# Moving layer-norm work of two batches between the attention stages and the MLP stage of a cross-attention block

## The chip, the cores and the metric

The kernel runs on one core of a Trainium2 chip. The metric is the device time of one execution in microseconds. Several executions are timed; the median is compared.

## The reference

A transformer block on x (4 batches x 512 rows x 512) with a context of the same shape, all in float32: layer norm 1, cross attention of 16 heads of width 32 with a mask, an output projection with residual, layer norm 2, an MLP of inner width 2048 with tanh-gelu, and a second residual.

```python
x = layer_norm(hidden_states, ln1_w, ln1_b)
q = heads(x @ q_w + q_b); k = heads(ctx @ k_w + k_b); v = heads(ctx @ v_w + v_b)
scores = where(mask, einsum('bhqd,bhkd->bhqk', q, k) * scale, min)
out = einsum('bhqk,bhkd->bhqd', softmax(scores), v)
hidden = merge(out) @ cproj_w + cproj_b + hidden_states
y = layer_norm(hidden, ln2_w, ln2_b)
return hidden + gelu(y @ fc_w + fc_b) @ proj_w + proj_b
```

## The kernel before

**Stages.** Attention is cut into 16 stages w = 4b + g, one per batch b and group g of four heads, and each stage into four units qt = 0 to 3 of 128 query rows. A unit is numbered u = 4w + qt, so stage 11 holds units 44 to 47 and stage 13 units 52 to 55. In a unit, `scores` (lines 255 to 272) makes four 128x512 score blocks on TensorE in one tile `sc` that has one buffer; VectorE adds the mask and takes the row minimum `mn` of the negated scores (line 266); ScalarE takes exponentials into `ptt` (line 270). `turn` (line 274) transposes 32x32 blocks into `tb` on VectorE (lines 285, 293, 294).

**Exchange.** Two units make a pair, numbered 2w + half. After a pair's second unit SP issues 16 transfers that finish the transposition between partitions (line 328). Pairs 25, 27, 29 and 31 land in the space of `xe`, pairs 1, 3, 5 and 7 in that of `gt`, and all others in the single buffer `pT`: the transfers of such a pair are issued only when the pair before it in `pT` has been attended. `attend` (line 331) multiplies the probabilities with v on TensorE (line 345, `av`) and normalises on VectorE (line 350, `oT`), after which a held pair may be issued. A pair is attended some units after it was made: pair 22 in unit 48, pair 23 in unit 50, pair 24 in unit 53, pair 26 in unit 57, pair 27 in unit 59.

**The order is written by hand.** The kernel uses a manual schedule: each engine executes in the order of the program text. Lists `first[w]` give the work that stands behind each unit; where it is a tuple, entry qt stands behind unit 4w + qt. In a unit come, in this order: attend (if due), scores, turn, the listed work. Such work is the k, q and v projections (`A`, lines 218 to 245), the output projection (`C`, line 386, with the residual addition on VectorE at line 387), layer norm 2 and parts of the MLP of earlier batches, which `some(n)` takes from one list in order: first layer pairs `fc` (line 528) and second layer tiles `proj` (line 536).

**Layer norm 2** of a batch has four parts. `stat2` takes mean and variance of a 128x512 tile on VectorE (lines 128, 129), `ln_rs` the inverse root on POOL (lines 134, 136), `norm2` subtracts and scales on VectorE (line 150), and `ln2_turn` transposes on TensorE (line 159) and applies weight and bias (lines 162, 164) into `yT`.

**Seven products.** The MLP replaces 8 block products by 7 (a Strassen-Winograd form), for which sums of blocks are needed: `y_sums` makes four 128x512 sums of `yT` on VectorE (line 452), into `ys` and in place; the weights' sums `wsum` are made on POOL during attention, and on VectorE behind it (`sum_wa`, lines 452 and 455 on `gt`). `fc_seven` (line 479) multiplies (line 491), copies one block p on ScalarE (line 494), adds the blocks on VectorE (line 455) and applies gelu on ScalarE (line 509). Gelu and the exponentials need different function tables, so ScalarE loads a table at each change.

**Bias rows.** `proj_bias` adds the second MLP bias to the residual tiles that stay on chip (batch one: two of four tiles) on POOL (line 357). `c_bias` does so with the projection's bias.

**Behind attention** `last_mlps` (line 575) runs the second half of batch one's MLP (first layer pairs c = 4 to 7), then all of batch two's and three's. Per pair: sums of the next pair's weights, seven products, the load of the weights after next; `g_sums` makes sums of gelu's outputs for every two pairs. In `project` the second layer follows; the transposes of the next batch's layer norm 2 (`turns2`) stand between its second and third product. Within batch two's first layer the kernel takes batch three's statistics and normalisations, by this block:

```python
if b == B - 2:
    for t in {0: (0,), 1: (1, 2), 3: (3,)}.get(c, ()):
        stat2(b + 1, t)
```

The lists that the change touches read before:

```python
first[11] = (..., t2[2:] + do(lambda: y_sums(1)) + pb_(1) + some(1) + h_(2, 2, 3, 0, 1))
first[13] = some(1), some(1) + stat(2, 0, 1), some(1) + stat(2, 2, 3) + rs(2), some(2)
first[14] = some(1) + norm(2, 0, 1), norm(2, 2, 3) + some(2), some(2), []
```

Of the kernel before, what the change touches and what calls it, by code (L numbers as in the profile page):

```python
# [52 lines left out]
def xattn_block(ctx: ExitStack, tc: tile.TileContext, x, encT, mask, q_w, k_w, v_w, c_w, fc_w, p_w, vecs, rows, out):  # L53
# [77 lines left out]
    def ln_rs(key):  # L131

        ve = small.tile([P, NT], F32, tag="ve", name=f"ve{key[0]}_{key[1]}")
        nc.gpsimd.tensor_scalar(ve, S["mv", key][:, :, 1], EPS, 1.0, ALU.add, ALU.mult)
        rs = small.tile([P, NT], F32, tag="rs", name=f"rs{key[0]}_{key[1]}")
        nc.gpsimd.tensor_tensor(rs, ve, nhalf, ALU.pow)
        S["rs", key] = rs
        if key in BY_ACT:
            nm = small.tile([P, NT], F32, tag="nm", name=f"nm{key[0]}_{key[1]}")
            nc.gpsimd.tensor_tensor(nm, S["mv", key][:, :, 0], rs, ALU.mult)  # L140
            nc.gpsimd.tensor_scalar(nm, nm, -1.0, 0.0, ALU.mult, ALU.add)
            S["nm", key] = nm
# [263 lines left out]
    def stat2(b, t):  # L406
        ln_stat((2, b), t, S["h", b, t])

    def norm2(b, t):
        h = S["h", b, t]  # L410
        y = tiles.tile([P, D], F32, tag="xn", name=f"xn2_{b}_{t}") if stays(b, t) else h
        S.setdefault(("yn", b), {})[t] = y
        ln_norm((2, b), t, y, h)
# [58 lines left out]
    def y_sums(b):  # L472
        y = y_blocks(b)
        b_sums(*y, ys[:, 0], ys[:, 1], y[1], ys[:, 2])
# [100 lines left out]
    def last_mlps():  # L575
        last, = pools(ctx, last=1)
        ps_last = ctx.enter_context(tc.tile_pool(name="ps_last", bufs=4, space=PSUM))
        ga = last.tile([P, NP, 2, L], F32, tag="ga", name="ga")
        gs = last.tile([P, 3, NP, HL], F32, tag="gs", name="gs")
        hl = last.tile([P, NT, D], F32, tag="hl", name="hl")  # L580
        for t in range(NT):
            S["hid", SPLIT + 1, t] = hl[:, t]
        p1p, u2p, u3p = (last.tile([P, 2, HL], F32, tag=n, name=n) for n in ("p1p", "u2p", "u3p"))

        def half_tile(name):
            return ps_last.tile([P, 2, HL], F32, tag="half", name=name)

        def g_sums(c):
            c = slice(c, c + 2)
            a11, a12, a21, a22 = (ga[:, c, k, j * HL : (j + 1) * HL] for j in range(2) for k in range(2))  # L590
            a_sums(a11, a12, a21, a22, gs[:, 0, c], gs[:, 1, c], a21, gs[:, 2, c])

        def fc_pair(b, c, sums):
            sums()
            fc_seven(b, c, ga[:, c], [wa[c % 2][:, i] for i in range(2)],
                     [ws[c % 2][:, i] for i in range(4)], half_tile)

        def project(b, pairs, sums, turns, middle):
            g11, g12, g21, g22 = (ga[:, :, k, j * HL : (j + 1) * HL] for j in range(2) for k in range(2))
            b11, b12, b21, b22 = (pb[:, :, k, j * HL : (j + 1) * HL] for k in range(2) for j in range(2))  # L600
            t1, t2, t3, t4 = pt[:, 0], pt[:, 1], b12, pt[:, 2]
            s1, s2, s3, s4 = gs[:, 0], gs[:, 1], g21, gs[:, 2]

            def product(o, a, w, ts_=range(2)):
                for t in ts_:
                    for c in pairs:
                        nc.tensor.matmul(  # L607
                            o[:, t], a[:, c, ts(t, P)], w[:, c], start=(c == pairs[0]), stop=(c == pairs[-1])
                        )

            def hid(i, j, t):
                return S["hid", b, 2 * i + t][:, j * HL : (j + 1) * HL]

            def join(engine, i, j, src):
                for t in range(2):
                    add(engine, hid(i, j, t), src[:, t], hid(i, j, t))

            def store(i, j):
                for t in range(2):
                    nc.sync.dma_start(out=out[b, ts(2 * i + t, P), j * HL : (j + 1) * HL], in_=hid(i, j, t))  # L620

            q1, q2 = (acc_half(f"{n}p_{b}") for n in ("q1", "q2"))
            product(q1, g11, b11)
            nc.scalar.copy(p1p, q1)
            sums()
            product(q2, g12, b21)
            turns()
            q3 = half_tile(f"q3p_{b}")
            product(q3, s4, b22)
            join(nc.vector, 0, 0, q2)  # L630
            join(nc.gpsimd, 0, 0, p1p)
            store(0, 0)
            q6 = acc_half(f"q6p_{b}")
            product(q6, s2, t2)
            add(nc.vector, u2p, q6, p1p)
            join(nc.vector, 0, 1, q3)
            q7 = half_tile(f"q7p_{b}")
            product(q7, s3, t3)
            add(nc.vector, u3p, q7, u2p)
            for i, j, src in ((0, 1, u2p), (1, 0, u3p), (1, 1, u3p)):  # L640
                join(nc.gpsimd, i, j, src)
            q5 = half_tile(f"q5p_{b}")
            product(q5, s1, t1)
            join(nc.vector, 0, 1, q5)
            join(nc.vector, 1, 1, q5)
            store(0, 1)
            store(1, 1)
            middle()
            q4 = half_tile(f"q4p_{b}"), acc_half(f"q4p_{b}")
            for t in range(2):  # L650
                product(q4[t], g22, t4, (t,))
                add(nc.vector, hid(1, 0, t), q4[t][:, t], hid(1, 0, t))
                nc.sync.dma_start(out=out[b, ts(2 + t, P), :HL], in_=hid(1, 0, t))

        half = FIRST * FQ // 2
        for b, pairs, new in (
            (SPLIT, range(half, NP), ()), (SPLIT + 1, range(NP), range(half)), (SPLIT + 2, range(NP), ())
        ):
            for c in pairs:
                if c in new:  # L660
                    for i in range(2):
                        nc.sync.dma_start(out=pb[:, c, i, :], in_=p_w[ts(2 * c + i, P), :])
                fc_pair(b, c, lambda: sum_wa(c + 1) if c + 1 < NP else None)
                if c + 2 < NP:
                    load_wa(c + 2)
                elif b + 1 < B:
                    load_wa(c + 2 - NP)
                if c % 2 == 0 and c != pairs[0]:
                    g_sums(c - 2)

                if b == B - 2:
                    for t in {0: (0,), 1: (1, 2), 3: (3,)}.get(c, ()):
                        stat2(b + 1, t)
                    if c == 3:
                        ln_rs((2, b + 1))
                    for t in {4: (0,), 5: (1, 2), 7: (3,)}.get(c, ()):
                        norm2(b + 1, t)
            g_sums(NP - 2)

            def sums(b=b, new=new):  # L680
                for c in new[::2]:
                    p_sums(c)
                if b + 1 < B:
                    load_hid(b + 1, range(NT))

            def turns(b=b):
                if b + 1 < B:
                    run(turns2(b + 1))
                if b == SPLIT:
                    load_xn(B - 1)  # L690

            def middle(b=b):
                if b + 1 < B:
                    y_sums(b + 1)
                    sum_wa(0)

            project(b, pairs, sums, turns, middle)
# [5 lines left out]
    def do(fn):  # L703
        return [(0.0, fn)]
# [93 lines left out]
    def some(n):  # L798
        taken = []
        while n > 0:  # L800
            n -= 1 if mlp[0][0] == CHAIN else 2
            taken.append(mlp.pop(0))
        assert n == 0
        return taken
# [4 lines left out]
    def h_(b, *ts_):  # L809
        return do(lambda: load_h(b, *ts_))  # L810
# [4 lines left out]
    def pb_(b):  # L815
        return do(lambda: proj_bias(b))

    def rs(b):
        return do(lambda: ln_rs((2, b)))

    def stat(b, *ts_):
        return do(lambda: [stat2(b, t) for t in ts_])

    def norm(b, *ts_):
        return do(lambda: [norm2(b, t) for t in ts_])
# [25 lines left out]
    t2 = turns2(1)  # L851
    first[11] = (
        [k, q] + stat(1, 0, 1, 2, 3) + rs(1), some(2) + norm(1, 0, 1, 2, 3), some(1) + t2[:2] + [v],
        t2[2:] + do(lambda: y_sums(1)) + pb_(1) + some(1) + h_(2, 2, 3, 0, 1)
    )

    k, q, v = A(15)
    c = C(2)
    first[12] = [k, q], cb(2) + [v], c[:2], c[2:]
    first[13] = some(1), some(1) + stat(2, 0, 1), some(1) + stat(2, 2, 3) + rs(2), some(2)  # L860
    first[14] = some(1) + norm(2, 0, 1), norm(2, 2, 3) + some(2), some(2), []
    first[15] = hid_(1, 2, 3) + some(2), [], some(2), some(1)

    for w in range(NW):
# [93 lines left out]
```

## Time and profile before

| What | Value |
|---|---|
| median of 3 runs | 818.54 us (818.28 to 819.71) |
| span of the profiled execution | 819.3 us, 12241 instructions; no other time is recorded for it |
| TensorE busy (PE) | 790.1 us, 96% |
| VectorE busy (DVE) | 586.2 us, 72% |
| ScalarE busy (ACT) | 335.1 us, 41% |
| GpSimd busy (POOL) | 134.4 us, 16% |
| mean granted TensorE clock | 0.988 |

The profile names lines of the kernel (L452 is line 452) and writes an operation as output <- inputs, with buffer numbers left out. In a timeline each row has its start from the span's beginning, its duration, engine, line and tiles, how many instructions are merged in it (x4), and in brackets the idle time in front of it with what ended it. PE is TensorE's matmul, PEld its weight load, SPq the issuing of transfers on SyncE's queue. Durations of neighbouring rows overlap a little, since instructions are pipelined.

### The profile page before, as it was taken

The numbers are of one execution on the slowest core, as the hardware profiler recorded it, in microseconds if no ns is written. First come the engines' busy times: TensorE is split into PE (matmuls) and PEld (weight loads), VectorE is DVE, ScalarE is ACT, GpSimd is POOL, SyncE is SP. The second block draws the span as 40 slices with busy tenths as digits, with TensorE's granted clock in tenths as the row PEclk, the third lists the DMA queues.
The fourth block names the chain that finished last, engine by engine and source line by source line (L and its number), as shares of the span: only waits on it lengthen the run. The fifth ranks groups of instructions, "written<-read, shape, count | busy, mean of one in ns | idle before, by whom it ended". The sixth has DMA issues, their size and how long they took to land.

```text
span 819.3 us, 12241 instructions
## 1 busy us (share of the span) xinstructions
PE 790.1 (96%) x4226; PEld 512.9 (63%) x4226; DVE 586.2 (72%) x1197; ACT 335.1 (41%) x745; POOL 134.4 (16%) x160
## 2 busy tenths in 40 slices
PE   9999999989999999999979977999999999999998
PEld 6545445555745645565444454545888888888887
DVE  3788998787889867679968988825647984368511
ACT  2566764656755636456434457500211221012200
POOL 1210033014121221000500240120041012200011
PEclk9999999999999999999999998999999999999999
DMA  9899989857878877777666897784244430023001
GB/s 330 275 242 239 231 208 258 225 127 182 210 211 223 208 207 194 176 202 161 161 157 193 213 254 174 177 249 142 77 129 143 140 117 13 26 78 91 0 14 39
DMA packets 60958, 137.17 MB, mean 167 GB/s; under 512 B 12464, under 2 KB 15664, under 8 KB 60768
## 3 DMA queue, kind: packets, MB, share of 16 engines
q1 hardware_dynamic: 59472, 132.43, 59.8%
q0 software_dynamic: 896, 2.82, 1.1%
q10 hardware_dynamic: 528, 1.14, 0.7%
q8 instruction: 34, 0.56, 0.3%
q14 instruction: 28, 0.23, 0.1%
HBM read 58.22 MB, written 6.82 MB: 79 GB/s over the span
## 4 chain that ended last, share of the span: by engine, by line
PE 79%; DVE 8%; SPq 6%; ACT 2%; DMA 2%; issue 2%; POOL 1%; DVEq 0%; POOLq 0%; ACTq 0%
PE q L491 20%; PE accp L539 10%; PE sc L262 7%; PE av L345 6%; PE accv L240 5%; PE acck L218 5%; SPq L328 5%; PE accc L386 5%; PE accq L228 4%; DVE ptt L266 3%; PE q4p L607 2%; PE q3p L607 2%; PE q7p L607 2%; PE q2p L607 2%; PE q5p L607 2%; PE q6p L607 2%
## 5 line engine op out<-in xcount | busy, mean ns | idle before, releaser
L270 ACT ACTIVATE ptt<-ptt,mn 128x512 f32<-128x512 f32 x256 | 181.7, 711 | 150.3 <-DVE mn L266 150.1
L266 DVE CUSTOM_DVE_ANT_0 ptt<-sc,mb 128x512 f32<-128x512 f32 x256 | 161.0, 685 | 30.9 <-PE sc L262 30.7
L285 DVE STREAM_TRANSPOSE tb<-ptt 128x1024 f32<-128x1024 f32 x96 | 119.1, 1242 | 14.2 <-ACT ptt L270 10.3
L539 PE MATMUL accp<-pbt,gt 128*128 128x512 f32 x192 | 86.8, 601 | 0.0
L262 PE MATMUL sc<-pbt 32*128 32x512 f32 x512 | 74.9, 655 | 9.7 <-DVE mn L266 7.6
L491 PE MATMUL q<-yT,gt 128*128 128x256 f32 x320 | 78.9, 379 | 0.0
L491 PEld LDWEIGHTS q<-yT,gt 128*128 128x128 f32 x320 | 60.8, 190 | 8.7 <-issue 0.5
L539 PEld LDWEIGHTS accp<-pbt,gt 128*128 128x128 f32 x192 | 35.1, 190 | 49.2 <-issue 45.8
L240 PEld LDWEIGHTS accv<-ptt,xe 128*128 128x128 f32 x512 | 58.7, 192 | 9.5 <-issue 6.7
L509 ACT ACTIVATE ga<-ga,vec 128x512 f32<-128x512 f32 x40 | 26.7, 715 | 85.6 <-DVE ga L455 85.6
L491 PE MATMUL q<-ys,gt 128*128 128x256 f32 x240 | 61.7, 379 | 0.0
L240 PE MATMUL accv<-ptt,xe 128*128 128x128 f32 x512 | 60.8, 277 | 0.0
L218 PE MATMUL acck<-xe,ptt 128*128 128x512 f32 x128 | 59.7, 610 | 0.0
L228 PE MATMUL accq<-xe,ptt 128*128 128x512 f32 x128 | 58.4, 599 | 0.0
L386 PE MATMUL accc<-wc,oT 128*128 128x512 f32 x128 | 56.6, 596 | 0.0
L345 PE MATMUL av<-pT,v 128*32 128x256 f32 x768 | 49.0, 398 | 7.8 <-DMA pT<-tb 6.0
L494 ACT COPY p<-q 128x256 f32<-128x256 f32 x32 | 11.4, 355 | 94.8 <-PE q L491 94.8
L491 PEld LDWEIGHTS q<-ys,gt 128*128 128x128 f32 x240 | 45.5, 190 | 6.6 <-DVE gt L452 0.4
L252 POOL TENSOR_TENSOR v<-v,row 128x512 f32<-128x512 f32 x16 | 20.4, 1274 | 173.6 <-ACT v L245 173.5
L270 ACT ACTIVATION_READ_ACCUMULATOR ptt<-ptt,mn 128x1 f32 x256 | 47.8, 187 | 0.0
L262 PEld LDWEIGHTS sc<-pbt 32*128 32x128 f32 x512 | 20.4, 186 | 42.8 <-issue 19.2
L345 PEld LDWEIGHTS av<-pT,v 128*32 128x32 f32 x768 | 24.4, 113 | 33.1 <-issue 17.0
(131 smaller groups left out, 1107.0 us busy)
## 6 DMA issues: line engine op xcount, KB each, us to landing
pT<-tb SPq DMA_DIRECT2D x384, 136.0 KB, 2.4
pbt<-p_w_dram SPq DMA_DIRECT2D x40, 256.0 KB, 3.1
gt<-fc_w_dram SPq DMA_DIRECT2D x40, 256.0 KB, 2.6
gt<-tb SPq DMA_DIRECT2D x64, 136.0 KB, 3.4
xe<-tb SPq DMA_DIRECT2D x56, 136.0 KB, 2.7
pbt<-fc_w_dram SPq DMA_DIRECT2D x24, 256.0 KB, 4.4
ptt<-k_w_dram SPq DMA_DIRECT2D x16, 256.0 KB, 3.9
xe<-encT_dram SPq DMA_DIRECT2D x16, 256.0 KB, 4.8
```

Source lines behind the costliest of these rows:

```text
L218: nc.tensor.matmul(acc, S["wk", w][:, d, :], eT[:, d, :], start=(d == 0), stop=(d == ND - 1))
L228: nc.tensor.matmul(acc, S["wq", w][:, d, :], xT[:, d, :], start=(d == 0), stop=(d == ND - 1))
L240: nc.tensor.matmul(acc[:, ts(t, P)], eT[:, d, ts(t, P)], S["wv", w][:, d, :], start=(d == 0), stop=(d == ND - 1),)
L262: nc.tensor.matmul(sc[:, h, :], qT[r, ts(qt, P)], kT[r, :], start=True, stop=True)
L266: nc.vector.tensor_tensor_reduce(out=s, in0=sc[:, h, :], in1=S["mb", w // NG], scale=1.0, scalar=FMAX, op0=ALU.add, op1=ALU.min, accum_out=mn,
L270: nc.scalar.activation(s, s, AF.Exp, bias=mn, scale=-1.0, accum_out=sums[:, qt, h : h + 1])
L285: nc.vector.transpose(*two_heads[k])
L345: nc.tensor.matmul(av[ts(h, HD), : 2 * P].rearrange(shape, **kw), v[:, t, ts(h, HD)], p[t][h], start=(t == 0), stop=(t == NT - 1),)
L386: nc.tensor.matmul(acc, S["oT", b][:, g, ts(t, P)], wc[:, g, :], start=(g == 0), stop=(g == NG - 1))
L491: nc.tensor.matmul(o, x[:, k], y[:, k], start=(k == 0), stop=(k == 1))
L539: nc.tensor.matmul(acc, gT[q % 2][:, k, ts(t, P)], S["pw", b, q * FQ + k], start=(k == 0), stop=(k == FQ - 1))
L607: nc.tensor.matmul(o[:, t], a[:, c, ts(t, P)], w[:, c], start=(c == pairs[0]), stop=(c == pairs[-1]))
```

## The change

Two moves. First, `y_sums(1)` leaves the work behind unit 47 and stands behind unit 52; `proj_bias(1)` leaves unit 47 too and stands behind unit 53. Second, layer norm 2 of batch two (four statistics in units 53 and 54, the inverse root in unit 54, the normalisations in units 56 and 57) leaves attention for the MLP stage: the statistics stand behind pairs 4 and 5 of batch one's first layer, the root behind pair 5, the normalisations behind pairs 6 and 7. The transposes of that layer norm stay where they were, in batch one's second layer. The orders of TensorE, ScalarE and SP do not change; VectorE's and POOL's do.

```diff
                 if c % 2 == 0 and c != pairs[0]:
                     g_sums(c - 2)
 
+                if b == SPLIT:
+                    for t in {4: (0, 1), 5: (2, 3)}[c] if c < 6 else ():
+                        stat2(b + 1, t)
+                    if c == 5:
+                        ln_rs((2, b + 1))
+                    for t in {6: (0, 1), 7: (2, 3)}[c] if c > 5 else ():
+                        norm2(b + 1, t)
                 if b == B - 2:
...
     first[11] = (
         [k, q] + stat(1, 0, 1, 2, 3) + rs(1), some(2) + norm(1, 0, 1, 2, 3), some(1) + t2[:2] + [v],
-        t2[2:] + do(lambda: y_sums(1)) + pb_(1) + some(1) + h_(2, 2, 3, 0, 1)
+        t2[2:] + some(1) + h_(2, 2, 3, 0, 1)
     )
...
-    first[13] = some(1), some(1) + stat(2, 0, 1), some(1) + stat(2, 2, 3) + rs(2), some(2)
-    first[14] = some(1) + norm(2, 0, 1), norm(2, 2, 3) + some(2), some(2), []
+    first[13] = some(1) + do(lambda: y_sums(1)), pb_(1) + some(1), some(1), some(2)
+    first[14] = some(1), some(2), some(2), []
```

## The prediction

> **What bounds the kernel now.** I read the page's chain first: it says which engine's work ends last.
>
> ```profile
> PE 79%; DVE 8%; SPq 6%; ACT 2%; DMA 2%; issue 2%; POOL 1%; DVEq 0%; POOLq 0%; ACTq 0%
> ```
>
> TensorE carries 79% of it, so a moved VectorE instruction matters only where the chain leaves TensorE. I then asked for the chain around each place that the change touches. A score unit is u = 4w + qt. The first place is the end of unit 47, where the sums of batch one (line 452) now stand. The columns are start, duration, what:
>
> ```profile
> 399.29 0.61 DVE ys L452
> ...
> 402.28 1.75 DVE ys L452
> 404.03 0.60 DVE h L543
> 404.64 0.80 DVE mb L198
> 405.44 0.35 DVE oT L350
> 405.80 0.51 SPq L328
> ...
> 415.24 2.36 DMA pT<-tb
> ```
>
> The chain runs through the four sums (399.29 to 404.03, 4.74 us), a residual addition, the mask and the normalising product oT of pair 22. That product frees the one pT buffer. SP then issues the 16 transfers of pair 23, and TensorE waits for the last of them. The timeline of TensorE shows that wait and those of units 53 to 60 (the bracket is the idle time before a row and its releaser):
>
> ```profile
> 408.27 1.14 PE L262 MATMUL sc<-pbt 32*128 32x512 f32 x8 [0.61 <-DVE mn L266]
> 409.34 3.84 PE L240 MATMUL accv<-ptt,xe 128*128 128x128 f32 x32
> 417.73 3.23 PE L345 MATMUL av<-pT,v 128*32 128x256 f32 x32 [4.56 <-DMA pT<-tb]
> ...
> 441.87 1.93 PE L345 MATMUL av<-pT,v 128*32 128x256 f32 x32
> ...
> 448.44 1.14 PE L262 MATMUL sc<-pbt 32*128 32x512 f32 x8
> ...
> 469.70 1.14 PE L262 MATMUL sc<-pbt 32*128 32x512 f32 x8
> ...
> 478.84 1.13 PE L491 MATMUL q<-yT,pbt 128*128 128x256 f32 x4 [0.68 <-ACT p L494]
> 481.05 1.13 PE L491 MATMUL q<-yT,pbt 128*128 128x256 f32 x4 [1.08 <-DVE gt L455]
> ...
> 485.48 1.03 PE L491 MATMUL q<-ys,pbt 128*128 128x256 f32 x4
> 488.98 3.45 PE L345 MATMUL av<-xe,v 128*32 128x256 f32 x32 [2.47 <-ACT p L494]
> ```
> ```profile
> 496.15 2.09 PE L262 MATMUL sc<-pbt 32*128 32x512 f32 x8 [2.66 <-DVE mn L266]
> 498.17 3.78 PE L491 MATMUL q<-yT,pbt 128*128 128x256 f32 x8
> ...
> 569.44 1.89 PE L491 MATMUL q<-yT,gt 128*128 128x256 f32 x8
> ```
> ```profile
> 496.00:500.00 4.00, 3.85 (x12) 2.03 (x13) 3.13 (x7) 2.58 (x8) 0.00 (x0) 0.50 0.09 33
> ```
>
> The same 32 attention products take 1.93 us at 441.87 but 3.23 and 3.45 after waits of 4.56 and 2.47. The table of stretches shows why: after the wait of 2.66 the granted clock (the third column from the end) is 0.50. After 0.61, 0.68 and 1.08 the rows are not longer. So each long wait costs its length and 1.3 to 1.5 us more.
>
> VectorE's timeline shows who makes these waits:
>
> ```profile
> 444.94 0.69 DVE L266 CUSTOM_DVE_ANT_0 ptt<-sc,mb 128x512 f32<-128x512 f32 x1 [0.65 <-PE sc L262]
> ...
> 447.39 0.08 DVE L266 DVE_READ_ACCUMULATOR2_ANT mn<- 128x1 f32 x1
> ...
> 472.93 1.00 DVE L150 TENSOR_SCALAR h<-h,mv,rs 128x512 f32<-128x512 f32 x2 [1.29 <-POOL rs L136]
> ...
> 474.18 0.68 DVE L266 CUSTOM_DVE_ANT_0 ptt<-sc,mb 128x512 f32<-128x512 f32 x1
> ...
> 479.44 0.96 DVE L150 TENSOR_SCALAR h<-h,mv,rs 128x512 f32<-128x512 f32 x2
> ...
> 492.50 0.42 DVE L350 TENSOR_TENSOR oT<-av,xe 128x256 f32<-128x256 f32 x1
> 493.56 0.69 DVE L266 CUSTOM_DVE_ANT_0 ptt<-sc,mb 128x512 f32<-128x512 f32 x1 [0.64 <-PE sc L262]
> ```
>
> In unit 57 the scores end at 469.70 + 1.14 = 470.84, but VectorE takes them up at 474.18, 3.34 us late: it waits 1.29 us for POOL's root and then normalises. Two more normalisations (479.44) stand in front of the additions that ScalarE's gelu, exponentials and copy p wait for, and p releases av at 488.98.
>
> **The change part by part.** Durations are from the one profiled execution, span 819.3 us; no time outside the span is recorded for it. The median, 818.54, lies 0.8 below that span; I subtract the sum from the median. The orders of TensorE, ScalarE and SP are unchanged.
>
> 1. *Sums leave unit 47.* The product oT, the 16 issues and the last landing come 4.74 us earlier, 417.73 becoming 412.99. TensorE is there at 409.34 + 3.84 - 0.61 = 412.57, because its 0.61 wait is caused by the same late VectorE. A wait of 0.4 remains, which no row shows to lower the clock, so 3.23 falls to 1.93. Gain: 4.74 + 1.30 = 6.0. Next in line is TensorE itself, 0.4 us behind.
>
> 2. *Sums arrive in unit 52, its bias additions in unit 53.* I need their price without POOL beside them, and POOL's own rows:
>
> ```profile
> 618.41 0.68 DVE L452 TENSOR_TENSOR ys<-yT 128x512 f32<-128x512 f32 x1
> ...
> 621.01 0.42 DVE L455 TENSOR_TENSOR gt<-gt 128x256 f32<-128x256 f32 x1
> ```
> ```profile
> 394.12 2.50 POOL L357 TENSOR_TENSOR h<-h,row 128x512 f32<-128x512 f32 x2
> 400.04 6.53 POOL L357 TENSOR_TENSOR h<-h,row 128x512 f32<-128x512 f32 x4 [3.43 <-DVE ys L452]
> ...
> 438.33 0.54 POOL L389 DMA_DIRECT2D xa<-h  x1 [1.34 <-DVE h L387]
> ```
>
> Batch two's sums take 618.41 to 621.01, 2.60 us; batch one's took 4.74 because two of them ran at 1.75 beside POOL's additions from 400.04. In the new place oT and the 4 score reductions of unit 53 are queued behind the sums. VectorE had 0.65 idle there, so the reductions begin 1.95 later and end at 447.47 + 1.95 = 449.4, on the old clock. TensorE wants to write the next scores at 448.44: a new wait of 1.0. The two bias additions, 2.5 us, have nothing left to wait for; POOL runs them right behind its store at 438.33, 438.9 to 441.4. The sums begin about 443.9, where oT stood, so I take no overlap. Lead: 6.0 - 1.0 = 5.0.
>
> Here the Trainium skill speaks against the move (SBUF — State Buffer, "Who interferes with whom"): a VectorE instruction with two inputs in SBUF and a GpSimd one that reads SBUF exclude each other. The 1.75 rows agree. By that rule alone, if they met, the price would be the third rival's; the rows put them 2.5 us apart.
>
> 3. *Statistics leave units 53 and 54, the root and two normalisations unit 56.* TensorE did not wait for the statistics; they were VectorE's lateness. Without them VectorE reaches unit 57's scores when they end: its lead grows by 3.34 to 8.3. TensorE's waits of 0.68 and 1.08 go, since p and the evictions come earlier too.
>
> 4. *Two normalisations leave unit 57:* 0.96 more, 9.3 for additions, gelu, exponentials and p. So av may start at 488.98 - 9.3 = 479.7. TensorE's own products end at 485.48 + 1.03 - 5.0 - 0.68 - 1.08 = 479.75: the wait of 2.47 is gone, and av takes 1.93.
>
> 5. *Unit 59.* With scores ready, VectorE's wait of 0.64 before 493.56 goes too: lead 9.3 + 0.64 = 9.95, and the scores of unit 60 come from 496.15 to 486.2. TensorE waits for them from 482.8, 3.4 us instead of 2.66: what is late next is VectorE, as before. The slow clock behind it I take as now. From there TensorE is the chain up to the last stage, and the lead stays.
>
> 6. *The work arrives in the MLP stage.* The rows of that stage, and the price of the same operations for batch three:
>
> ```profile
> 578.24 0.42 DVE L455 TENSOR_TENSOR gt<-gt 128x256 f32<-128x256 f32 x1 [1.87 <-DMA gt<-fc_w_dram]
> ...
> 584.38 0.43 DVE L455 TENSOR_TENSOR gt<-gt 128x256 f32<-128x256 f32 x1 [1.93 <-DMA gt<-fc_w_dram]
> ...
> 593.81 0.69 DVE L455 TENSOR_TENSOR ga<-q,ga 128x512 f32<-128x512 f32 x1 [0.58 <-PE q L491]
> ...
> 634.43 0.69 DVE L128 BATCH_NORM_STATS2 st<-hn 128x6 f32<-128x512 f32 x1
> ...
> 636.04 0.39 DVE L455 TENSOR_TENSOR gt<-gt 128x256 f32<-128x256 f32 x1
> ```
>
> Two statistics take 636.04 - 634.43 = 1.61 us. The pairs fall into the idle 1.87 before 578.24 and 1.93 before 584.38, where VectorE waits for weights. Two normalisations (0.96) fall in front of pair 7's additions; the idle 0.58 before 593.81 gives back part of it, and what remains, 0.4, stands in front of one addition and its gelu only. Near the lower end, by the idle rows, I take +0.1, with bounds 0 and 5.1 (2 x 1.61 + 2 x 0.96, no cover at all).
>
> Sum: -9.95 + 0.1 = -9.85. 818.54 - 9.85 = 808.7 us.
>
> The clock after unit 60's wait is the open price. Rows 496.15 and 498.17 took 2.09 and 3.78 where full speed gives 1.14 (448.44) and 1.89 (569.44): 2.8 us lost. After the other long waits 1.3 and 1.5 were lost, so it may cost 1.5 less, or twice that at the far end.
> The Trainium skill (TensorE: Matmul & The Clock Gate, "What's actually happening") says that the monitor's window of 3.4 us is free-running, so the same wait can cost more or less; the rows agree in that three waits cost three amounts. By it the sum could move either way by a window, about 1.7 us as an estimate.
>
> **The rivals.**
>
> *The second half does not come (10%).* If units 57 to 60 keep their waits because ScalarE's table changes or an exchange, not VectorE, ends last, only the lead of 5.0 stays: 813.5. The releaser p after a run of VectorE work without idle speaks against it.
>
> *Unit 50's wait stays (5%).* If the issues of pair 23 hung on SP and not on oT, step 1 gives nothing, and TensorE keeps 9.85 - 6.0 = 3.9: 814.7. Against it: SP starts at 405.80, right as oT ends.
>
> *The sums meet POOL in unit 52 (8%).* Two of them at 1.75 instead of 0.65 add 2.2 to the wait of 1.0; at 3.2 the clock falls, 1.4 more: 808.7 + 3.6 = 812.3. It decides if POOL is 2.5 us later than I place it.
>
> *VectorE becomes the bound of the MLP stage: slower (4%).* If the cover of step 6 fails, 5.1 us land on the path. Then the four sums that follow slide wholly into POOL's additions for the next batch, 1.1 more each, 4.4. TensorE's wait costs the clock up to 2.8. That is 12.3 against a gain of 9.95: 818.54 + 2.35 = 820.9. It decides from the point where the backlog at pair 7 exceeds about 10 us; the two idle times of 1.9 speak against it.
>
> **How the numbers follow.** Forecast 73%; the rivals 10, 5, 8 and 4%. About 0.2% is what a measurement of this kernel can tell from no change. Faster takes the forecast and three rivals, less some doubt: 94%; same 2%; slower 4%. The range goes down to 808.7 - 2.8 = 805.9 (no slow clock at unit 60) and up to 813.5, the first rival.
>
> **What would show it.** In the changed kernel av of pair 23 comes at about 413 with a wait under 1 us and takes 1.9; the sums in unit 52 take 2.6; a new wait of about 1.0 for mn stands in unit 54; the waits of 0.68, 1.08 and 2.47 are gone; the wait before unit 60 is about 3.4; the first products of the MLP stage start near 559.5 instead of 569.4, and the stage keeps its length within 0.3. A wait above 2 us in units 48 to 57, sums at 1.75, or a longer MLP stage would prove the step wrong.

## The result, and the profile after

The changed kernel takes 809.67 us (median of 4 runs, 809.09 to 810.49) against 819.12 us for the kernel before in the same comparison: 9.45 us less, ratio 0.9888, 95% interval 0.9871 to 0.9904. The forecast was 808.7, with a range of 805.9 to 813.5. The profiled execution's span went from 819.3 to 808.7.

The chain on the page of the changed kernel has the same owner as before:

```profile
PE 78%; DVE 7%; SPq 7%; DMA 4%; issue 2%; ACT 2%; POOL 0%; DVEq 0%; POOLq 0%; ACTq 0%
```

POOL's 1% is gone. In the kernel before, the chain ran through POOL from 467.97 to 472.90: four sums of weights, the issue of a store, and behind them the inverse root, for which VectorE waited 1.29 us.

```profile
467.97 0.75 POOL wsum L455
...
471.86 1.04 POOL rs L136
```

In the changed kernel the chain in order of time around unit 50 shows what took the place of the sums, SP's issues and the last transfer:

```profile
407.38 1.07 PE sc L262 x8
408.45 3.77 PE accv L240 x32
412.21 1.88 PE av L345 x32
414.09 1.07 PE sc L262 x8
```

TensorE follows itself; no wait is left there. TensorE's timeline at the places that the prediction named:

```profile
397.31 1.93 PE L345 MATMUL av<-pT,v 128*32 128x256 f32 x32
...
412.16 1.93 PE L345 MATMUL av<-pT,v 128*32 128x256 f32 x32
...
442.38 1.14 PE L262 MATMUL sc<-pbt 32*128 32x512 f32 x8 [0.75 <-DVE mn L266]
...
478.74 1.93 PE L345 MATMUL av<-xe,v 128*32 128x256 f32 x32 [0.40 <-ACT p L494]
...
485.16 2.09 PE L262 MATMUL sc<-pbt 32*128 32x512 f32 x8 [3.42 <-DVE mn L266]
487.18 3.78 PE L491 MATMUL q<-yT,pbt 128*128 128x256 f32 x8
```
```profile
558.56 1.89 PE L491 MATMUL q<-yT,gt 128*128 128x256 f32 x8
...
584.75 2.43 PE L607 MATMUL q1p<-pbt,ga 128*128 128x256 f32 x10 [0.56 <-ACT ga L509]
...
606.25 3.62 PE L607 MATMUL q4p<-ptt,ga 128*128 128x256 f32 x16
```

The old waits of 0.68, 1.08 and 4.56 us are gone, the one of 2.47 is down to 0.40, and a new one of 0.75 has come. VectorE's rows and POOL's:

```profile
398.82 0.68 DVE L543 TENSOR_TENSOR h<-accp,h 128x512 f32<-128x512 f32 x1
399.42 0.42 DVE L198 TENSOR_SCALAR mb<-m 128x512 f32<-128x512 uint8 x1
399.75 0.42 DVE L350 TENSOR_TENSOR oT<-av,pT 128x256 f32<-128x256 f32 x1
```
```profile
436.94 0.67 DVE L452 TENSOR_TENSOR ys<-yT 128x512 f32<-128x512 f32 x1
...
439.46 0.42 DVE L350 TENSOR_TENSOR oT<-av,pT 128x256 f32<-128x256 f32 x1
...
464.85 0.69 DVE L266 CUSTOM_DVE_ANT_0 ptt<-sc,mb 128x512 f32<-128x512 f32 x1 [0.65 <-PE sc L262]
```
```profile
432.01 2.52 POOL L357 TENSOR_TENSOR h<-h,row 128x512 f32<-128x512 f32 x2
```

The sums take 436.94 to 439.46, 2.52 us, and POOL ended its bias additions at 434.53, 2.4 us earlier. At unit 57 (464.85) it is VectorE that waits for the scores now, not the other way round.

**A measure that is finer than the time.** Single runs scatter over several us: in one comparison 25 runs of the kernel before lie between 816.73 and 823.04. The traces show one source: all kernels here have the same program up to the work behind unit 47, and yet av of pair 22 starts anywhere from 393.9 to 397.8 us. For small steps I therefore read the stretch from the start of that av to the q4 products of batch one's MLP. In the kernel before its ends are:

```profile
397.58 1.93 PE L345 MATMUL av<-pT,v 128*32 128x256 f32 x32
...
595.32 2.43 PE L607 MATMUL q1p<-pbt,ga 128*128 128x256 f32 x10 [0.25 <-ACT ga L509]
...
616.81 3.62 PE L607 MATMUL q4p<-ptt,ga 128*128 128x256 f32 x16
```

Each stretch is from one trace, and the two traces of the changed kernel differ by 0.55 in it: 0.44 lies in the slow clock behind unit 60, 0.1 in the wait before the second layer. Up to the scores of unit 60 they agree, with 87.85 and 87.84 us; small effects ahead of unit 60 are read there.

| Kernel | median, us | before, us | ratio (95%) | stretch, us |
|---|---|---|---|---|
| before | | 819.12 | | 219.23 |
| changed | 809.67 | 819.12 | 0.9888 (0.9871 to 0.9904) | 208.94 |
| changed, again | 808.04 | 818.66 | 0.9864 (0.9836 to 0.9892) | 208.39 |
| sums only | 814.03 | 819.01 | 0.9948 (0.9927 to 0.9969) | 214.73 |
| layer norm only | 814.29 | 819.01 | 0.9944 (0.9923 to 0.9965) | 215.16 |
| batch two's bias later | 815.92 | 819.01 | 0.9956 (0.9932 to 0.9980) | 216.87 |
| sums left out | 807.38 | 819.01 | 0.9859 (0.9827 to 0.9890) | 208.21 |
| sums split | 808.80 | 819.16 | 0.9882 (0.9858 to 0.9907) | 209.05 |
| normalisations late | 809.24 | 819.16 | 0.9886 (0.9859 to 0.9913) | 208.54 |
| pairs 2, 3 earlier | 811.17 | 819.16 | 0.9911 (0.9882 to 0.9939) | 210.10 |
| all three | 810.33 | 819.16 | 0.9901 (0.9874 to 0.9928) | 210.63 |
| sums between, norms late | 807.86 | 818.66 | 0.9872 (0.9851 to 0.9894) | 207.72 |

### The profile page after: what moved, and what is told of

Its sections match the earlier page's. It is cut to its first block, busy times and chain, and to the rows that moved or that the text cites. A ratio compares the mean times of both kernels' runs of the same rounds, so it can differ in the third digit from the quotient of the medians.

```text
span 808.7 us, 12244 instructions
## 1 busy us (share of the span) xinstructions
PE 786.8 (97%) x4226; PEld 512.2 (63%) x4226; DVE 584.8 (72%) x1197; ACT 335.3 (41%) x745; POOL 132.9 (16%) x160
## 3 DMA queue, kind: packets, MB, share of 16 engines
q10 hardware_dynamic: 528, 1.14, 0.7%
## 4 chain that ended last, share of the span: by engine, by line
PE 78%; DVE 7%; SPq 7%; DMA 4%; issue 2%; ACT 2%; POOL 0%; DVEq 0%; POOLq 0%; ACTq 0%
PE q L491 20%; PE accp L539 9%; PE sc L262 6%; PE av L345 6%; SPq L328 6%; PE accc L386 6%; PE accv L240 5%; PE acck L218 5%; PE accq L228 4%; DVE ptt L266 3%; PE q4p L607 2%; PE q3p L607 2%; PE q5p L607 2%; PE q6p L607 2%; PE q2p L607 2%; PE q7p L607 2%
## 5 line engine op out<-in xcount | busy, mean ns | idle before, releaser
L262 PE MATMUL sc<-pbt 32*128 32x512 f32 x512 | 74.9, 655 | 10.6 <-DVE mn L266 8.5
L228 PEld LDWEIGHTS accq<-xe,ptt 128*128 128x128 f32 x128 | 23.6, 190 | 32.4 <-issue 30.4
```

Of the source, the lines that this page charges most:

```text
L228: nc.tensor.matmul(acc, S["wq", w][:, d, :], xT[:, d, :], start=(d == 0), stop=(d == ND - 1))
L262: nc.tensor.matmul(sc[:, h, :], qT[r, ts(qt, P)], kT[r, :], start=True, stop=True)
```

## The experiments

**One move at a time.** The first kernel has the sums and bias additions moved and layer norm 2 of batch two still in attention (against the kernel before):

```diff
-        t2[2:] + do(lambda: y_sums(1)) + pb_(1) + some(1) + h_(2, 2, 3, 0, 1)
+        t2[2:] + some(1) + h_(2, 2, 3, 0, 1)
...
-    first[13] = some(1), some(1) + stat(2, 0, 1), some(1) + stat(2, 2, 3) + rs(2), some(2)
+    first[13] = some(1) + do(lambda: y_sums(1)), pb_(1) + some(1) + stat(2, 0, 1), some(1) + stat(2, 2, 3) + rs(2), some(2)
     first[14] = some(1) + norm(2, 0, 1), norm(2, 2, 3) + some(2), some(2), []
```

> Only the first move: batch one's sums and bias additions in units 52 and 53, batch two's layer norm 2 still in attention. Theory (two separate waits, each made by VectorE): the wait of 4.56 us before av of pair 23 goes, a wait of 0.8 in unit 54 comes, as in the changed kernel; but the statistics stand in front of the reductions again and the normalisations wait for POOL's root (about 469.2 by the changed kernel's POOL rows), so the lead of about 6 shrinks to some 3.7 by unit 57: about 815.4 us, 814 to 816. Rival A (the layer norm's move brings nothing): the whole gain, about 809.7. Rival B (the layer norm's move is all of it): no gain, 819.

The second has the layer norm moved and the sums at home (against the changed kernel):

```diff
-        t2[2:] + some(1) + h_(2, 2, 3, 0, 1)
+        t2[2:] + do(lambda: y_sums(1)) + pb_(1) + some(1) + h_(2, 2, 3, 0, 1)
...
-    first[13] = some(1) + do(lambda: y_sums(1)), pb_(1) + some(1), some(1), some(2)
+    first[13] = some(1), some(1), some(1), some(2)
     first[14] = some(1), some(2), some(2), []
```

> Only the second move: batch two's layer norm 2 behind attention, batch one's sums and bias additions back in unit 47. Theory: the wait of 4.56 at pair 23 stays with its slow clock; VectorE's lateness of 3.34 in unit 57, the normalisations' 0.96 and the 0.64 of unit 59 go, 0.3 is paid in the MLP stage: gain 4.6, about 814.5 us, 813.5 to 815.5. The waits of 0.68, 1.08 and 2.47 are gone, the one before unit 60 is about 3.4. Rival A: 819 or slightly more. Rival B: about 809.7.

Measured: 814.03 and 814.29, 4.98 and 4.72 less than before. Both rivals fall: neither move is the whole gain. TensorE's waits with the sums alone:

```profile
442.60 1.14 PE L262 MATMUL sc<-pbt 32*128 32x512 f32 x8 [0.74 <-DVE mn L266]
...
450.01 1.14 PE L262 MATMUL sc<-pbt 32*128 32x512 f32 x8 [0.77 <-DVE mn L266]
...
484.23 3.55 PE L345 MATMUL av<-xe,v 128*32 128x256 f32 x32 [2.47 <-ACT p L494]
```
with the layer norm alone:
```profile
414.07 3.64 PE L345 MATMUL av<-pT,v 128*32 128x256 f32 x32 [4.56 <-DMA pT<-tb]
...
482.10 1.93 PE L345 MATMUL av<-xe,v 128*32 128x256 f32 x32 [0.40 <-ACT p L494]
```

Each kernel keeps exactly the waits that belong to the move it lacks: 2.47 in the first, 4.56 in the second. By the medians the two gains add up within the scatter: 9.70 together against 9.45 and 10.62 for both moves at once. By the stretch they gain 4.50 and 4.07, together 8.57, and both moves at once gain 10.29 (10.84 in the second trace). The first kernel accounts for 0.77 of the rest: with the sums in unit 52 the statistics make a wait in unit 55, which needs both to exist. Another 1.0 is the clock in the second kernel, and nothing of the moves: behind the same wait of 4.56 the 32 products took 3.64 here and 3.23 in the kernel before, and up to the output projection's first product it was 5.20 against 4.24.

**Are the sums slow because of POOL?** The kernel before, with the bias additions of batch two behind the v product of stage 15:

```diff
-    first[12] = [k, q], cb(2) + [v], c[:2], c[2:]
+    first[12] = [k, q], [v] + cb(2), c[:2], c[2:]
```

> The kernel before with one edit: the four bias additions of batch two stand behind stage 15's v product on POOL, so that they come after 413 us and not beside batch one's sums, which stay in unit 47. Theory (two of the four sums and the mask are slow because POOL reads beside them): the sums take 2.6 and not 4.74, the mask 0.42 and not 0.88, so oT and the transfers of pair 23 come 2.6 earlier, the wait of 4.56 falls to about 2: 816.5 us, or 815.2 if the clock does not fall then. Rival (two sums are slow by their own operands): they stay at 1.75 and the time at 819.

VectorE's timeline of this kernel, and TensorE's wait:

```profile
399.00 0.68 DVE L452 TENSOR_TENSOR yT<-yT 128x512 f32<-128x512 f32 x1
399.61 0.68 DVE L452 TENSOR_TENSOR ys<-yT,ys 128x512 f32<-128x512 f32 x1
400.21 0.68 DVE L543 TENSOR_TENSOR h<-accp,h 128x512 f32<-128x512 f32 x1
400.81 0.41 DVE L198 TENSOR_SCALAR mb<-m 128x512 f32<-128x512 uint8 x1
```
```profile
413.53 3.37 PE L345 MATMUL av<-pT,v 128*32 128x256 f32 x32 [2.64 <-DMA pT<-tb]
```

All four sums take 0.68 and the mask 0.41 (0.88 in the kernel before). The wait falls from 4.56 to 2.64 and not to 2, since TensorE's own short wait in front of it went too; the clock still falls. The stretch is 2.36 shorter, the time 3.1. From av of pair 22 to av of pair 23 it takes 17.55 instead of 20.15, where the changed kernel takes 14.85: moving POOL's additions away brings 2.60 of the 5.30 by itself. About half of the delay that the sums made in unit 47 was their meeting, and the mask's, with POOL.

**What do the sums cost in unit 52?** The changed kernel without them:

```diff
-    first[13] = some(1) + do(lambda: y_sums(1)), pb_(1) + some(1), some(1), some(2)
+    first[13] = some(1), pb_(1) + some(1), some(1), some(2)
```

> The changed kernel with batch one's four sums left out altogether (the MLP of batch one works on old sums). Theory (in unit 52 the sums cost only the new wait of 0.75 in unit 54, and the chain behind it follows TensorE): 0.75 less than the changed kernel, about 808.9 us. Rival (they lie wholly beside other work there): the changed kernel's 809.7. Rival (they cost their full 2.6): 807.1.

Measured 807.38, with the kernel before at 819.01. The time is 2.3 lower than the first and 0.7 lower than the second measurement of the changed kernel, too coarse to exclude the rival of 2.6 by itself. The trace excludes it: the wait of 0.75 is gone, no other wait of attention changed, and up to the scores of unit 60 it takes 87.11 instead of 87.85, 0.74 less, which is the wait alone. (The whole stretch is 0.2 to 0.7 shorter than the two of the changed kernel; q1's wait in the MLP stage is 0.90 here, longer than their 0.56 and 0.47.)

**Can the sums be had for nothing?** Two sums behind unit 50 and two behind unit 51 (`y_half(b, n)` is one half of `y_sums`):

```diff
+    first[12] = [k, q], cb(2) + [v], c[:2] + do(lambda: y_half(1, 0)), c[2:] + do(lambda: y_half(1, 1))
...
+    first[13] = some(1), pb_(1) + some(1), some(1), some(2)
```

> The changed kernel with batch one's four sums split: two behind unit 50, two behind unit 51, where VectorE's rows show idle times of 1.58 and 1.19 us in front of TensorE's output projection; nothing in unit 52. Theory (the sums cost what does not fit into VectorE's idle time in front of the next scores): the wait of 0.75 in unit 54 goes and none takes its place; from av of pair 22 to the q4 products of batch one's MLP 208.2 us instead of 208.94, as with the sums left out; time 0.7 less than the changed kernel. Rival (VectorE's total work up to unit 57 counts, not its place): no difference.

The stretch is 209.05, no shorter, and up to the scores of unit 60 it is even 1.45 longer (89.30). My theory missed; VectorE's timeline tells why, with POOL's beside it and the wait that followed:

```profile
429.46 0.68 DVE L452 TENSOR_TENSOR yT<-yT 128x512 f32<-128x512 f32 x1
430.06 3.39 DVE L452 TENSOR_TENSOR ys<-yT,ys 128x512 f32<-128x512 f32 x1
```
```profile
430.40 2.50 POOL L357 TENSOR_TENSOR h<-h,row 128x512 f32<-128x512 f32 x2
```
```profile
435.95 1.14 PE L262 MATMUL sc<-pbt 32*128 32x512 f32 x8 [0.64 <-DVE mn L266]
...
441.71 1.14 PE L262 MATMUL sc<-pbt 32*128 32x512 f32 x8 [0.99 <-DVE mn L266]
```

The fourth sum met both bias additions and took 3.39 instead of 0.68: the collision that the prediction's third rival had feared for unit 52. The two waits that followed, and one of 0.44 ahead of them for the transfers of pair 23, are together 1.3 us more than the one wait of 0.75. The whole stretch hides this by luck of the clock:

```profile
484.49 1.14 PE L262 MATMUL sc<-pbt 32*128 32x512 f32 x8 [3.42 <-DVE mn L266]
485.56 3.51 PE L501 MATMUL q<-yT,pbt 128*128 128x256 f32 x8
```

Behind the same wait of 3.42 the scores of unit 60 still ran at full speed here (1.14 and not 2.09), and up to the next av it took 9.00 us, against 9.92 to 10.42 in the six other traces with that wait. So the first split is worse than the sums in unit 52, not equal to it.

The sums also stood behind the second residual addition of their unit, when the idle time was over. A later kernel puts them in front of it, so that they end before POOL begins, and takes in the next experiment's edit too:

```diff
+    first[12] = [k, q], cb(2) + [v], c[:1] + do(lambda: y_half(1, 0)) + c[1:2], c[2:3] + do(lambda: y_half(1, 1)) + c[3:]
...
+    first[13] = some(1), pb_(1) + some(1), some(1), some(2)
```

> The changed kernel with two edits: batch one's sums split again, but in front of the last residual addition of units 50 and 51, so that they lie in VectorE's idle time there and end before POOL's bias additions begin; and all four normalisations of batch two behind pair 7. In the first split the fourth sum took 3.39 us because it met POOL's bias additions. Theory (place in idle time and no POOL beside it): all four sums take about 0.68, no wait for mn in units 53 and 54, q1 waits 0.25; from av of pair 22 to the q4 products about 207.9 us against 208.94 in the changed kernel; time 1.0 less. Rival (VectorE's load up to unit 57 counts, wherever the sums are): a wait of about 0.75 before some scores stays, and the stretch is 208.5 or more.

> The changed kernel once more, unedited, on the same chip and in the same rounds, as the measure for the kernel with split sums and late normalisations: the stretch from av of pair 22 to the q4 products is 208.9 us again within 0.5, the time 809 to 810.

```profile
427.77 0.67 DVE L452 TENSOR_TENSOR yT<-yT 128x512 f32<-128x512 f32 x1
428.36 0.68 DVE L452 TENSOR_TENSOR ys<-yT,ys 128x512 f32<-128x512 f32 x1
429.04 0.69 DVE L387 TENSOR_TENSOR h<-accc,h 128x512 f32<-128x512 f32 x1
430.07 0.69 DVE L266 CUSTOM_DVE_ANT_0 ptt<-sc,mb 128x512 f32<-128x512 f32 x1 [0.34 <-PE sc L262]
```

All sums are at 0.68, VectorE still waits for the next scores, and TensorE has no wait between unit 48 and unit 58. The stretch is 207.72, 0.7 and 1.2 less than the two of the changed kernel. Up to the scores of unit 60 it takes 87.03, 0.82 less, as little as with the sums left out (87.11): placed here the sums cost nothing. The time was expected 1.0 lower; 807.86 against 808.04 for the changed kernel beside it cannot show so little. The unedited changed kernel itself came out at 808.04 where 809 to 810 was expected, and its stretch, 208.39, missed 208.9 by a hair more than the 0.5 allowed: both measures scatter by more than I had said.

**What does the MLP stage pay?** All four normalisations behind pair 7:

```diff
-                    for t in {6: (0, 1), 7: (2, 3)}[c] if c > 5 else ():
+                    for t in range(NT) if c == 7 else ():
```

> The changed kernel with all four normalisations of batch two behind pair 7 of batch one's first layer, none behind pair 6. Theory (what the MLP stage pays is the two normalisations in front of pair 7's additions): the wait of the second layer's q1 for gelu goes from 0.56 back to 0.25, and the stage is 0.3 shorter by the trace; the time cannot tell that from nothing. Rival (it is VectorE's load as a whole, with POOL's additions beside it): the wait stays or a new one stands before the transposes.

```profile
582.57 2.43 PE L607 MATMUL q1p<-pbt,ga 128*128 128x256 f32 x10 [0.24 <-ACT ga L509]
```

The wait of q1, the first product of the second layer, is 0.24, and the time from its first row to q4 is 23.20 as in the kernel before; in the changed kernel it is 23.52. All three kernels with this edit have 0.24, the six traces with two normalisations behind pair 6 have 0.47 to 0.90. The theory holds: the two normalisations in front of pair 7's additions are the whole price. The time moved by less than can be told.

**Can the waits before units 60 and 62 be filled?** Batch one's pairs 2 and 3 behind units 59 and 60:

```diff
-    first[14] = some(1), some(2), some(2), []
-    first[15] = hid_(1, 2, 3) + some(2), [], some(2), some(1)
+    first[14] = some(1), some(2), some(2), some(2)
+    first[15] = hid_(1, 2, 3) + some(2), some(1), some(1), some(1)
...
     attend(NW - 1, 0)
-    run(some(2))
+    run(some(1))
```

> The changed kernel with batch one's first-layer pairs 2 and 3 one stage unit block earlier: pair 2 behind unit 59 and pair 3 behind unit 60 instead of units 60 and 62, then one second-layer tile each behind units 61, 62, 63. Theory (TensorE waits 3.42 and 2.65 us before the scores of units 60 and 62 with a slow clock after each, because it has no other work there): both waits shrink, TensorE is about 7 us ahead in its work at the end of unit 63, and the gain is what the exchange of the last pair lets through, 4 to 6.5: about 803 to 806 us. Rival (VectorE and ScalarE, with their table loads, end last in these units, and the wait comes back before the last av): less than 1 us gained.

```profile
495.47 1.93 PE L345 MATMUL av<-pT,v 128*32 128x256 f32 x32 [2.46 <-ACT p L494]
...
526.50 3.64 PE L345 MATMUL av<-pT,v 128*32 128x256 f32 x32 [5.43 <-DMA pT<-tb]
```

The time is 811.17 and the stretch 210.10, longer than in the changed kernel, so the theory missed. The rival has the outcome right, but only part of the reason. The waits of 3.42 and 2.65 are gone and ScalarE's copy p comes late (2.46), as it said. The larger wait, 5.43 for the transfers of pair 30, has another source, which SP's issues and the chain show:

```profile
506.41 17.92 SPq L328 DMA_DIRECT2D pT<-tb  x16
```
```profile
520.77 2.39 DMA xe<-tb
...
523.18 2.57 DMA pT<-tb
```

The 16 issues of pair 30 take 17.92 us; in the changed kernel they take 10.04. SP had issued 14 by 515.2, then waited 8.0 us until a transfer of pair 31, issued from ScalarE's queue, had landed, and issued the last two at 523.18. The changed kernel has a like wait (10.6 us) at the same place in SP's order, behind the 20th transfer after pair 29's. There it stands in front of two loads of second layer weights, which TensorE did not wait for; the edit moved two such loads ahead of pair 30, and so the wait fell between pair 30's own transfers. Issued without that wait, the last two would have landed near 519 (an estimate: 515.2 + 1.2 for two issues + 2.4), before TensorE's products ahead of that av end at 521.07. So this run does not show that TensorE's idle time before units 60 and 62 is worth nothing; the same fill with the loads behind pair 30 was not run, and what SP's wait is for in the program stays open.

> The three edits together (sums split, normalisations late, pairs 2 and 3 earlier). Theory: the gains add, about 1.0 less than the kernel with pairs 2 and 3 earlier, 802 to 805. Rival: as much as the largest single one.

The three edits together give 810.33 and a stretch of 210.63, with the same wait for pair 30 (5.38). The 802 to 805 of the theory is missed, because the pairs' move that it builds on brought nothing, and the rival is missed too: by the medians the gain is smaller than with the normalisations or the split alone. The sums are split here in the first way, and the fourth takes 3.39 beside POOL again: up to av of pair 27 it takes 82.47 against 81.52 with the pairs alone. The late normalisations do add (q1 waits 0.24 instead of 0.60). The time, 0.8 lower than with the pairs alone, is within the scatter.

## Why the prediction was right, point by point

1. *Sums leave unit 47: right, 0.6 too small.* Forecast 6.0. From av of pair 22 to av of pair 23 it was 20.15 before and is 14.85, 5.3 less, and the products take 1.93 instead of 3.23: 6.6. Counted from av of pair 22, oT came 5.34 earlier and not 4.74: 0.46 of the difference is the mask, which fell from 0.88 to 0.42 as well. I had not seen that the mask too ran beside POOL; the kernel with batch two's bias later shows it. The 0.4 of wait that I had left is therefore gone. TensorE and the transfers are close to each other there: in the kernel with the sums split a wait of 0.44 came back.

2. *A new wait in unit 54: right.* Forecast 1.0, measured 0.75. POOL's bias additions ended 2.4 us ahead of the sums (forecast 2.5), so the third rival stayed away; the split sums show that it was real, at 3.39 for one sum.

3. and 4. *Unit 57 and the copy p: right.* VectorE waits 0.65 for the scores of unit 57 instead of being 3.34 late. The waits of 0.68 and 1.08 are gone, 2.47 became 0.40 where I had forecast none, and av takes 1.93. The first rival (5.0 only) falls with it; the kernel with the layer norm alone shows the second half by itself.

5. *Unit 60: right.* Wait 3.42 (forecast 3.4), and the slow clock behind it as before: 2.09 and 3.78.

6. *The MLP stage: right in kind, too small.* Forecast 0.1, measured 0.31 (q1's wait from 0.25 to 0.56). The statistics did fit: the idle 1.87 and 1.93 became 0.43 and 0.16.

```profile
567.54 0.43 DVE L455 TENSOR_TENSOR gt<-gt 128x256 f32<-128x256 f32 x1 [0.43 <-DMA gt<-fc_w_dram]
...
573.52 0.42 DVE L455 TENSOR_TENSOR gt<-gt 128x256 f32<-128x256 f32 x1 [0.16 <-DMA gt<-fc_w_dram]
...
580.29 1.00 DVE L150 TENSOR_SCALAR h<-h,mv,rs 128x512 f32<-128x512 f32 x2
```

For the normalisations I had worked out 0.4 in front of the last addition and then taken 0.1 against my own sum. From its first products to the end of the span the stage takes 250.1 instead of 249.9, within the 0.3 that I had allowed.

The start of the MLP stage came at 558.56 where 559.5 was forecast; 0.3 of that lay ahead of unit 48. The sum of steps, 9.85, stands against 10.29 by the stretch and 9.45 by the medians. That it lies between them is partly luck: steps 1 and 2 were better by 0.6 and 0.25, step 6 worse by 0.2, and the medians of the same two kernels gave 10.62 when measured again. The slower rival needed a backlog of 10 us; q1 waited 0.56.

The clock stayed the loose term. The Trainium skill (TensorE: Matmul & The Clock Gate, "What's actually happening") calls the monitor's window free-running. The runs fit that, though none of them shows the window itself: waits of 2.47 cost the 32 products 3.45, 3.51 and 3.55 in three kernels, and a wait of 2.46 cost them nothing (1.93, row 495.47, at a granted clock of 1.00). Behind unit 60's wait of 3.42 the clock cost up to 1.4 us more in one kernel than in another (10.42 against 9.00), of the size that the prediction had left open.

## What to carry to other kernels

Follow the chain back from a wait until it leaves the engine that waits: here a 4.56 us wait for a transfer was four sums on another engine, in front of the product that freed the buffer. Price a moved instruction by what it meets in its new place, not by its mean: a sum of 0.68 us took 1.75 or 3.39 beside GpSimd additions. And before giving an idle TensorE more to do, see which engine ends last there, and which transfers the moved work takes along: two weight loads that moved in SP's order put a wait of 8.0 us between the transfers that TensorE needed.

## What the runs showed of the hardware that was not expected

The mask, one tensor-scalar instruction with a single 8-bit input in SBUF, took 0.88 us beside POOL's additions and 0.41 to 0.42 without. The Trainium skill (SBUF — State Buffer, "Who interferes with whom") lists tensor-scalar among the operations that can take the shared ports; the rows agree.

A VectorE sum lost 1.1 us to each meeting in unit 47, where four POOL additions and the sums alternated, but 2.7 us in the split kernel, where its record spans two additions in a row (430.40 to 432.90) and ends 0.55 us behind the second. The same four POOL additions took 6.53 us beside the sums and 4.96 alone:

```profile
400.21 4.96 POOL L357 TENSOR_TENSOR h<-h,row 128x512 f32<-128x512 f32 x4 [6.45 <-DVE oT L350]
```
